# Layer 0's output products moved into layer 1, and the gates spread by sixteen transfers to every sixteenth partition

## The chip, the cores and the metric

The kernel runs on one core of one Trainium2 chip. The metric is the time of one execution on the device, in microseconds (us). Of three runs of the kernel before the median is 1395.56 us (1394.31 to 1398.51). The profile is of a further execution, which took 1393.95 us.

Names of engines: PE is TensorE (PEld its weight loads), DVE is VectorE, ACT is ScalarE, POOL is GpSimd. SP is SyncE, which issues nearly all of this kernel's transfers (SPq marks the issuing instructions).

## What is computed

A network of four layers on x of 8 batches of 512 tokens of 128 channels, in fp32. Each layer adds an attention-like block and a feed-forward block to x, each after a layer norm. The change touches the feed-forward block of layer 0, a mixture of experts for each head of each token:

```python
def _L0_ffn_ref(x, Wm, bm, expert_emb, W1, b1, W2, b2, Wo, bo):
    H, E, K = (8, 16, 2)                      # heads, experts, experts kept
    h = x @ Wm + bm
    t = h.reshape(bs * L_ * H, HD)            # HD = 16 channels a head
    w = softmax(t @ expert_emb)
    topw, topi = top_k(w, K)
    hmid = gelu(einsum('td,edi->tei', t, W1) + b1)
    eo = einsum('tei,eio->teo', hmid, W2) + b2
    comb = (take(eo, topi) * topw).sum(axis=1)
    return comb.reshape(bs, L_, d) @ Wo + bo

x = x + _L0_ffn_ref(_layernorm(x), ...)
```

The kernel computes all 16 experts for every token and multiplies each with a gate, the softmax weight where the expert is among the best two and zero elsewhere. Layer 1 is linear attention with a gated feed-forward and a few chosen tokens, layers 2 and 3 follow; the change does not touch what they compute.

## The kernel before

The residual lies in SBUF as x0 to x7, one tile for each batch. The program is written out by hand in order (`tc.manual_schedule`): what the code issues first on an engine runs first there, and an instruction that waits holds up everything behind it on its engine. SP is such a queue too. Each transfer that SP issues also waits until the transfer eight before it on SP has landed, so at most eight are under way.

**Phase A** (to about 100 us) is layer 0's attention and the preparation of its experts: two software pipelines over the eight batches (`run`, L498 to L535), each a list of stages with a lag. `scale(b, own)` (L343) applies a layer norm to the four 128-token tiles of a batch, `own` of them on ACT and the rest on POOL; the second list calls it with all four on ACT (L520). `logits` and `exponentials` (L440) write the exponentials of the softmax into the accumulator `acc` of the batch, which is free at that time.

**Gates.** `choice(b)` (L442 to L481) makes the gates of a batch on DVE in 13 steps, transposes them and writes them to DRAM as `gates[b]`, 128 rows (8 heads by 16 experts) of 512 tokens, in four transfers of 64 KB (L477). `spread(b, k)` (L543 to L554) reads the gates of experts 4k to 4k+3 back into a tile `gs` of 128 partitions by 4 experts by 512 tokens. In SBUF the partitions are 8 heads of 16 channels, so each head's 8 KB (4 experts by 512 tokens) goes to 16 neighbouring partitions. That is one transfer for each head: eight transfers of 16 partitions by 8 KB, 128 KB each. The first spread of all, (0, 0), is cut in two by experts and has sixteen transfers of 64 KB. The tile has three buffers. There are 32 spreads of 1 MB, four for each batch; `fetch` (L666) issues the next one when its batch's gates are written and the buffer three back has been used.

**Units.** The 128 pairs (batch, expert) are units. `first_half` (L556) makes four matmuls `ps<-h,w` and the Gelu on ACT (L569 of 512 columns, L570 of 1536). `second_half` (L573), issued two units later, makes four matmuls `ps<-hm,w`, then DVE `pr = (ps + b2) * gs` (L582), then POOL `acc += pr` (L588; expert 0 writes `acc` directly). Of the last unit of all, `pr` is kept instead of added. Between units `side` (L650) puts one piece of other work: a step of the next batch's `choice`, or of the index places and first norms of layer 1.

**Finish.** `finish(b)` (L590) multiplies a batch's `acc` with `wo` (four matmuls `ps<-blob_f,acc` at L250, in `by_token`) and adds the product to x on DVE (L274, `add_to_residual`). In the loop over units it stands in the unit of expert 4 of the next batch, between that unit's first half and the second half of the one two before, and takes its PSUM bank from one of the two three-bank tiles (`threes`) that the first halves use in turn. The last one, `finish(7)`, stands behind the loop and has eight matmuls, since it adds the kept `pr` as a second term.

**Layer 1** follows at once: a pipeline over i = 0 to 7 of the stages at L1217 to L1238, each with a lag, so that batch i + lag is worked on. `stats` has lag 2, `scale` lag 1, `project_q` and `project_kv` lag 0. A tile `nought` of zeros (L1253) is written to two DRAM buffers at the layer's start (L1256, L1261). Layers 2 and 3 come after it.

Of the kernel before, what the change touches and what calls it, by code (L numbers as in the profile page):

```python
# [25 lines left out]
P = 128  # L26
D = 128
# [137 lines left out]
def body(ctx, tc, dram, spans, x_in, ib, it, ic, ei, out):  # L165
# [111 lines left out]
        return t[:, j * P : (j + 1) * P]  # L277


    def layer0():  # L280


# [5 lines left out]
        with ExitStack() as st:  # L288
# [4 lines left out]
            emb = once.tile([P, 8, 16], F32, tag="emb", name="emb")  # L293
            emb_f = emb.rearrange("p h e -> p (h e)")
            h = once.tile([P, NB, TB], F32, tag="h", name="h")
            acc = once.tile([P, NB, TB], F32, tag="acc", name="acc")
            depth = once.tile([P, NB, TB], F32, tag="depth", name="depth")
            gates = [tc.dram_tile([P, TB], F32, name=f"gates{b}") for b in range(NB)]
            G = J * 8
# [40 lines left out]
            def stats(b):  # L340
                l0[b]["by"] = stats_of(x[b], J)

            def scale(b, own=3):  # L343
                l0[b]["xn"] = xn = norm.tile([P, J, D], F32, tag="xn", name="xn")
                nb, rs = l0[b]["by"]
                scaled(xn, x[b], (nb, rs), own)
                for j in range(own, J):
                    r1, n1 = rs[:, j : j + 1], nb[:, j : j + 1]
                    nc.gpsimd.tensor_scalar(xn[:, j, :], x[b][:, j, :], r1, n1, ALU.mult, ALU.add)

            def biased(b, bias):
                nc.gpsimd.tensor_tensor(
# [84 lines left out]
                nc.vector.tensor_tensor(by_expert(depth, b), pl3, over(mx), ALU.subtract)  # L437

            def exponentials(b):
                nc.scalar.activation(acc[:, b, :], depth[:, b, :], AF.Exp)  # L440

            def choice(b):  # L442


                d, ex = by_expert(depth, b), by_expert(acc, b)
                place, top, sm = small("place"), small("top"), small("sm")
                eq, one, left = big("eq"), big("one"), big("left")
                nc.vector.scalar_tensor_tensor(eq, d, 0.0, rank, ALU.is_equal, ALU.mult)
                yield "V"
                nc.vector.tensor_reduce(place, eq, AX.X, ALU.max)  # L450
                yield "V"
                nc.vector.tensor_tensor(one, eq, over(place), ALU.is_equal)
                yield "V"
                nc.vector.scalar_tensor_tensor(left, one, -1e30, d, ALU.mult, ALU.add)
                yield "V"
                nc.vector.tensor_reduce(top, left, AX.X, ALU.max)
                yield "V"
                nc.vector.tensor_tensor(eq, left, over(top), ALU.is_equal)
                nc.gpsimd.tensor_tensor(eq, eq, rank, ALU.mult)
                yield "V"  # L460
                nc.vector.tensor_reduce(sm, ex, AX.X, ALU.add)
                nc.vector.reciprocal(sm, sm)
                nc.gpsimd.tensor_tensor(ex, ex, over(sm), ALU.mult)
                yield "V"
                nc.vector.tensor_reduce(place, eq, AX.X, ALU.max)
                yield "V"
                nc.vector.tensor_tensor(one, eq, over(place), ALU.is_equal)
                yield "V"
                nc.vector.scalar_tensor_tensor(left, one, -1e30, left, ALU.mult, ALU.add)
                yield "V"  # L470
                nc.vector.scalar_tensor_tensor(left, left, -1e29, ex, ALU.is_le, ALU.mult)
                yield "V"
                g = big("turned").rearrange("p g e -> p (g e)")
                nc.vector.transpose(g, left.rearrange("p g e -> p (g e)"))
                to = gates[b].rearrange("(c r) (j a s) -> a r j c s", c=4, j=J, a=4)
                for a in range(4):
                    nc.sync.dma_start(  # L477
                        to[a], g[32 * a : 32 * (a + 1), :].rearrange("r (j c s) -> r j c s", j=J, c=4)
                    )
                written.add(b)  # L480
                yield "V"  # L481
# [7 lines left out]
            with (  # L489
                tc.tile_pool(name="a0h", bufs=1) as hp,  # L490
                tc.tile_pool(name="a0", bufs=2) as ap,
                psum({"one": 8}),
                tc.manual_schedule(),
            ):
                hs = [hp.tile([P, NB, TB], F32, tag=f"h{k}", name=f"h{k}") for k in range(3)]
                bst = [hp.tile([P, NB, 6], F32, tag=f"bst{k}", name=f"bst{k}") for k in range(3)]

                def run(stages, iterations):  # L498
                    for i in iterations:
                        for f, lag in stages:  # L500
                            if 0 <= i + lag < NB:
                                f(i + lag)

                run(
                    (
                        (scale, 2),
                        (stats, 3),
                        (turned, 1),
                        (project, 0),
                        (lambda b: biased(b, "bp"), -2),  # L510
                    ),
                    range(-3, NB + 2),
                )
                keep_clock(22)
                sc, bi = batch_norm()
                expand()
                run(
                    (
                        (turned, -2),
                        (lambda b: scale(b, J), -1),  # L520
                        (turn_v, 3),
                        (logits, -3),
                        (attended, 0),
                        (stats, 0),
                        (spikes, 4),
                        (gram, 2),
                        (gram_out, 1),
                        (hidden, -2),
                        (exponentials, -3),
                        (lambda b: chosen(3), -4),  # L530
                        (lambda b: biased(b, "bo"), -1),
                        (lambda b: keep_clock(6), -3 - NB // 2),
                    ),
                    range(-4, NB + 3),
                )  # L535
                chosen(20)
# [6 lines left out]
            def spread(b, k):  # L543

                gs = wp.tile([P, 4, TB], F32, tag="gs", name="gs", bufs=3)
                src = gates[b].rearrange("(h k e) t -> k h e t", h=8, k=4)[k]
                n = 2 if (b, k) == (0, 0) else 4
                for e in range(0, 4, n):
                    for hd in range(8):
                        nc.sync.dma_start(  # L550
                            gs[16 * hd : 16 * (hd + 1), e : e + n, :],
                            src[hd, e : e + n, :].unsqueeze(0).to_broadcast([16, n, TB]),
                        )
                return gs  # L554

            def first_half(b, e):  # L556
# [16 lines left out]
            def second_half(b, e, hm, gs):  # L573
                po = bank()
                for i in range(4):
# [2 lines left out]
                        w2[:, e, :, :].rearrange("p a o -> p (a o)"),  # L578
                        hm[:, i, :],
                    )  # L580
                pr = acc[:, b, :] if e == 0 else wp.tile([P, TB], F32, tag="pr", name="pr")
                nc.vector.scalar_tensor_tensor(  # L582
                    pr, po, f0["b2"][:, e : e + 1], gs, ALU.add, ALU.mult
                )
                if (b, e) == (NB - 1, 15):
                    l0[b]["last"] = pr
                elif e > 0:
                    nc.gpsimd.tensor_tensor(acc[:, b, :], acc[:, b, :], pr, ALU.add)  # L588

            def finish(b):  # L590
                terms = [(lambda j: acc[:, b, j * P : (j + 1) * P], f0["wo"])]
                if "last" in l0[b]:
                    terms.append((lambda j: cols(l0[b]["last"], j), f0["wo"]))
                add_to_residual(b, by_token(terms, None))

            def places():

# [45 lines left out]
            with tc.manual_schedule():  # L643
# [36 lines left out]
                def second(n):  # L680

                    if n >= 2:
                        b, e = units[n - 2]
                        second_half(b, e, hms.pop(n - 2), gs[(n - 2) // 4][:, e % 4, :])
                        fetch(n - 1)
                    for _ in range(1 if n > 1 else 5):
                        side("V", n)

                for n in range(len(units) + 2):
                    first(n)  # L690
                    if n >= len(units):

                        banks["own"] = threes[0][:, 1 + n - len(units), :]
                        second(n)
                        banks.pop("own")
                        continue

                    banks["own"] = threes[(n + 1) % 2][:, 0, :]
                    b, e = units[min(n, len(units) - 1)]
                    if e == 4 and b > 0:  # L700
                        finish(b - 1)
                    else:
                        side("P", n)
                    banks.pop("own")
                    second(n)
                finish(NB - 1)
                n = 1000
                while kinds.get(1) != "end":
                    side("V", n)
# [121 lines left out]
    def layer1():  # L831
# [9 lines left out]
        with tc.tile_pool(name="l1", bufs=2) as wp, tc.tile_pool(name="l1c", bufs=1) as once:  # L841
# [372 lines left out]
            def chosen_put():  # L1214
# [11 lines left out]
                (f_scale, -3),  # L1226
                (q_map, 0),
                (project_kv, 0),
                (z_turn, -7),
                (output, -2),  # L1230
                (k_map, 0),
# [7 lines left out]
            with tc.manual_schedule():  # L1239
# [10 lines left out]
                for k, name in enumerate(("eb1", "eb2")):  # L1250
                    lo, hi = spans["rows"][name]
                    nc.sync.dma_start(ebs[:, k, :], dram["rows"][:, lo:hi].partition_broadcast(P))
                nought = once.tile([P, J, D], F32, tag="nought", name="nought")  # L1253
                nc.gpsimd.memset(nought, 0.0)
                for b in range(1, NB):
                    nc.sync.dma_start(  # L1256
# [1421 lines left out]
```

## Time and profile before

| what | us |
|---|---|
| median of three runs | 1395.56 |
| the profiled execution | 1393.95 |
| its span in the trace | 1392.2 |
| first transfer of spread (0, 0) is issued | 97.8 |
| last transfer of the last spread is issued | 364.9 |
| last gating on DVE (L582) starts | 383.76 |
| first matmul of layer 1 | 386.24 |
| one iteration of layer 1 | 7.49 |

The span is what the trace covers. All times inside the kernel are counted from its start. A line of a group gives the code line, engine, operation and tiles (output, then inputs), the count, and behind it the busy time, the mean of one in ns, and the idle time of the engine just before with what ended it. In a view by stretches each engine has its busy time in the stretch; behind them stand the granted PE clock, the mean busy share of the 16 DMA engines and the GB/s that they moved. The granted clock of PE is full over the whole span (0.998 on average).

The unit stage lies between about 102 and 386 us. One unit takes 2.07 us there, and a batch of 16 takes 34.06 us (the first) to 34.9 us, with one unit of 3.49 us in each, the one that holds a `finish`.

### The profile page before, as it was taken

The page shows a single profiled execution, that of the slowest core. Times are in us where ns is not written, and L with a number is a line of the kernel's source. Part 1 is how long each engine was busy: PE and PEld are TensorE (multiplying, and loading weights), DVE is VectorE, ACT ScalarE, POOL GpSimd, SP SyncE. Part 2 cuts the span into 40 slices and gives each one's busy share as a digit, 9 for nine tenths or more (in the row PEclk, how much of TensorE's full clock was granted, in tenths as well). Part 3 has the DMA queues.
Part 4 walks back from the last instruction along what each step waited for, and adds up shares of the span by engine and source line. Part 5 has one row for each costly group of instructions (what it writes and reads, how often), then busy time and mean ns, then how long its engine had stood idle before and what let it go on. Part 6 is the DMA issues. An engine that isn't in the chain of part 4 may idle for free.

```text
span 1392.2 us, 33106 instructions
## 1 busy us (share of the span) xinstructions
PE 1327.5 (95%) x12935; PEld 706.1 (51%) x12935; DVE 1014.3 (73%) x2148; ACT 1014.6 (73%) x2060; POOL 642.4 (46%) x748
## 2 busy tenths in 40 slices
PE   7889999999989999999999999999999999999997
PEld 3762222222267655547447545555555545555576
DVE  6785556666467778863783778888788797887876
ACT  7869999999978656665684686787767867667632
POOL 6645666666632533330472353353443634424432
PEclk9999999999999999999999999999999999999999
DMA  5019999999681010031211101101011010010000
GB/s 180 1 27 139 141 126 127 132 127 133 85 272 32 28 40 24 16 108 33 60 31 38 45 2 22 30 2 33 20 22 24 9 33 20 19 27 9 2 8 16
DMA packets 100713, 78.14 MB, mean 56 GB/s; under 512 B 52717, under 2 KB 93581, under 8 KB 96206
## 3 DMA queue, kind: packets, MB, share of 16 engines
q1 hardware_dynamic: 98828, 72.10, 28.3%
q0 software_dynamic: 1152, 2.36, 0.6%
q8 instruction: 102, 1.67, 0.6%
q10 hardware_dynamic: 578, 1.57, 0.3%
q14 instruction: 53, 0.43, 0.1%
HBM read 59.03 MB, written 16.97 MB: 55 GB/s over the span
## 4 chain that ended last, share of the span: by engine, by line
PE 52%; ACT 22%; DVE 19%; issue 3%; POOL 2%; DMA 1%; SPq 1%; DVEq 0%; ACTq 0%; POOLq 0%
PE ps L250 41%; PE ps L1556 8%; ACT hm L570 6%; ACT ex L1635 5%; DVE nm L1629 5%; ACT hm L569 3%; ACT prod L2023 2%; PE ps L2206 1%; DVE fa L1395 1%; DVE acc L2009 1%; DVE s L732 1%; ACT h L389 1%; DVE fa L1379 1%; DVE fsc L1374 1%; ACT q L1517 1%
## 5 line engine op out<-in xcount | busy, mean ns | idle before, releaser
L1635 ACT ACTIVATE ex<-ps,nm 128x512 f32<-128x512 f32 x512 | 345.2, 687 | 172.6 <-DVE nm L1629 170.2
L1629 DVE TENSOR_REDUCE nm<-ps 128x2 f32<-128x1024 f32 x256 | 301.1, 1211 | 41.9 <-PE ps L250 41.5
L250 PE MATMUL ps<-q,k 64*64 64x512 f32 (+1 forms) x2240 | 258.3, 565 | 7.4 <-ACT ex L1635 5.4
L250 PE MATMUL ps<-ex,vs 128*64 128x512 f32 x1024 | 233.9, 599 | 1.1 <-DVE sm L1649 1.1
L1650 POOL TENSOR_TENSOR vs<-v,sm 128x256 f32<-128x256 f32 x128 | 78.6, 614 | 296.6 <-DVE sm L1649 269.6
L588 POOL TENSOR_TENSOR acc<-acc,pr 128x512 f32<-128x512 f32 x119 | 165.6, 1391 | 93.8 <-DVE pr L582 85.8
L1556 PE MATMUL ps<-xt,blob_a 64*64 64x512 f32 x912 | 207.8, 589 | 0.5 <-SPq L1523 0.5
L570 ACT ACTIVATE hm<-ps,blob_f 128x1536 f32<-128x1536 f32 x128 | 196.2, 1533 | 0.0
L582 DVE SCALAR_TENSOR_TENSOR pr<-ps,blob_f,gs 128x512 f32<-128x512 f32 x120 | 90.1, 750 | 93.7 <-PE ps L250 72.1
L250 PEld LDWEIGHTS ps<-q,k 64*64 64x64 f32 x2240 | 74.6, 132 | 150.5 <-ACT ex L1635 77.6
L250 PE MATMUL ps<-h,w 32*128 32x512 f32 x1024 | 148.3, 643 | 1.1 <-ACT hm L569 0.6
L250 PEld LDWEIGHTS ps<-ex,vs 128*64 128x64 f32 x1024 | 68.1, 137 | 152.9 <-issue 126.7
L250 PE MATMUL ps<-hm,w 128*32 128x512 f32 x1024 | 136.9, 607 | 2.3 <-DVE pr L582 2.2
L2024 POOL TENSOR_TENSOR acs<-acs,prod 128x512 f32<-128x512 f32 x96 | 124.0, 1292 | 23.9 <-ACT prod L2023 19.4
L1556 PE MATMUL ps<-blob_a,ct 64*64 64x128 f32 x1824 | 118.6, 269 | 0.0
L1556 PE MATMUL ps<-blob_a,xt 64*64 64x128 f32 x1824 | 118.6, 269 | 0.0
L1556 PEld LDWEIGHTS ps<-blob_a,ct 64*64 64x64 f32 x1824 | 106.3, 133 | 0.0
L1635 ACT ACTIVATION_READ_ACCUMULATOR ex<-ps,nm 128x1 f32 x512 | 104.9, 205 | 0.0
L1556 PEld LDWEIGHTS ps<-blob_a,xt 64*64 64x64 f32 x1824 | 103.0, 133 | 0.0
L569 ACT ACTIVATE hm<-ps,blob_f 128x512 f32<-128x512 f32 x128 | 88.0, 687 | 13.3 <-PE ps L250 13.2
L250 PEld LDWEIGHTS ps<-h,w 32*128 32x128 f32 x1024 | 41.0, 184 | 109.1 <-ACT hm L569 100.5
L1556 PEld LDWEIGHTS ps<-xt,blob_a 64*64 64x64 f32 x912 | 61.7, 133 | 32.2 <-issue 28.7
(373 smaller groups left out, 2204.5 us busy)
## 6 DMA issues: line engine op xcount, KB each, us to landing
gs<-gates SPq DMA_DIRECT2D x248, 128.0 KB, 7.4
ht<-turned_h SPq DMA_DIRECT2D x20, 180.0 KB, 3.0
turned_h<-hb SPq DMA_DIRECT2D x40, 88.0 KB, 2.3
blob_f<-in_f SPq DMA_DIRECT2D x1, 2560.0 KB, 9.0
blob_a<-in_a SPq DMA_DIRECT2D x1, 2056.0 KB, 13.5
x<-in_x SPq DMA_DIRECT2D x8, 256.0 KB, 5.8
gates<-turned SPq DMA_DIRECT2D x32, 64.0 KB, 4.7
slots_in<-nought SPq DMA_DIRECT2D x8, 256.0 KB, 4.8
```

Source lines behind the costliest of these rows:

```text
L250: nc.tensor.matmul(out_, lhs, rhs, start=start, stop=stop)
L389: nc.scalar.activation(hk, hk, AF.Sigmoid, bias=bi[:, k : k + 1], scale=sc[:, k : k + 1])
L569: nc.scalar.activation(hm[:, 0, :], p1, AF.Gelu, bias=bias)
L570: nc.scalar.activation(hm[:, 1:, :], p3, AF.Gelu, bias=bias)
L582: nc.vector.scalar_tensor_tensor(pr, po, f0["b2"][:, e : e + 1], gs, ALU.add, ALU.mult)
L588: nc.gpsimd.tensor_tensor(acc[:, b, :], acc[:, b, :], pr, ALU.add)
L1556: ins = nc.tensor.matmul(*args, **kw).ins
L1629: nc.vector.tensor_reduce(nm, ps, AX.X, ALU.max, negate=True)
L1635: nc.scalar.activation(ex[kt][:, i, :], ps[:, i, :], AF.Exp, bias=nm[:, i : i + 1], accum_out=sm[:, kt, i : i + 1],)
L1650: nc.gpsimd.tensor_tensor(vs[:, tiles, :, :], vs_[n][:, tiles, :].rearrange("p j (i n) -> p j i n", i=2), sm[:, tiles, :].unsqueeze(3).to_ ...
L2023: nc.scalar.activation(p, src, AF.Copy, scale=w)
L2024: nc.gpsimd.tensor_tensor(t["acs"], t["acs"], p, ALU.add)
```

## The change

It has five parts, all in one diff.

1. `acc` is no longer one tile of layer 0. Batches 0 to 2 have tiles of their own there; batches 3 to 7 share `last_acc` in a pool that lives through layer 1. `finish` is defined outside layer 0. The kept `pr` of the last unit is gone: POOL adds it to `acc` as for any unit, and every `finish` has four matmuls.
2. In the unit loop only `finish(0)` and `finish(1)` remain. `finish(2)` stands behind the second half of unit 126, in the drain of the loop. `finish(3)` to `finish(7)` are a stage of layer 1 with lag 3, behind `project_kv`.
3. A spread, other than (0, 0), is sixteen transfers in place of eight. Transfer r takes the same 64 KB of all eight heads, and puts head j's 8 KB on partition r + 16 j: eight partitions of 8 KB, 64 KB. SP's issues of gates rise from 264 to 512 (16 and 496).
4. `scale` in phase A's second list puts three of the four tiles on ACT and the fourth on POOL, as the first list does.
5. In the first two units four and two pieces of `side` work run in place of five and five. `nought` takes its buffer from a tile of another name.

```diff
+    acc = []
+    last_acc = first.tile([P, NB - 3, TB], F32, tag="acc", name="acc")
+
+    def finish(b):
+        wo = f0["wo"]
+        add_to_residual(b, by_token([(lambda j: cols(acc[b], j), wo)], None))
+
     def layer0():
...
-            acc = once.tile([P, NB, TB], F32, tag="acc", name="acc")
+            acc.extend(once.tile([P, TB], F32, tag=f"acc{b}", name="acc") for b in range(3))
+            acc.extend(last_acc[:, b, :] for b in range(NB - 3))
...
-                        (lambda b: scale(b, J), -1),
+                        (scale, -1),
...
                 src = gates[b].rearrange("(h k e) t -> k h e t", h=8, k=4)[k]
-                n = 2 if (b, k) == (0, 0) else 4
-                for e in range(0, 4, n):
-                    for hd in range(8):
-                        nc.sync.dma_start(
-                            gs[16 * hd : 16 * (hd + 1), e : e + n, :],
-                            src[hd, e : e + n, :].unsqueeze(0).to_broadcast([16, n, TB]),
-                        )
+                if (b, k) == (0, 0):
+                    for e in (slice(0, 2), slice(2, 4)):
+                        for hd in range(8):
+                            nc.sync.dma_start(
+                                gs[16 * hd : 16 * (hd + 1), e, :],
+                                src[hd, e, :].unsqueeze(0).to_broadcast([16, 2, TB]),
+                            )
+                else:
+                    for r in range(16):
+                        nc.sync.dma_start(gs[r::16, :, :], src)
...
-                if (b, e) == (NB - 1, 15):
-                    l0[b]["last"] = pr
-                elif e > 0:
-                    nc.gpsimd.tensor_tensor(acc[:, b, :], acc[:, b, :], pr, ALU.add)
+                if e > 0:
+                    nc.gpsimd.tensor_tensor(acc[b], acc[b], pr, ALU.add)
...
-                    for _ in range(1 if n > 1 else 5):
+                    for _ in range((4, 2)[n] if n < 2 else 1):
                         side("V", n)
...
                     if n >= len(units):
-                        banks["own"] = threes[0][:, 1 + n - len(units), :]
+                        if n > len(units):
+                            banks["own"] = bank("first")
                         second(n)
+                        if n == len(units):
+                            banks["own"] = threes[0][:, 0, :]
+                            finish(2)
                         banks.pop("own")
                         continue
...
-                    if e == 4 and b > 0:
+                    if e == 4 and 0 < b < 3:
                         finish(b - 1)
...
-                finish(NB - 1)
...
                 (project_kv, 0),
+                (lambda b: b > 2 and finish(b), 3),
                 (z_turn, -7),
...
-                nought = once.tile([P, J, D], F32, tag="nought", name="nought")
+                nought = wp.tile([P, J, D], F32, tag="zo", name="nought")
```

More of the change, by code (lines that the diff above doesn't have):

```diff
@@ L341, in stats, with scale @@
                 l0[b]["by"] = stats_of(x[b], J)
-            def scale(b, own=3):
+            def scale(b):
                 l0[b]["xn"] = xn = norm.tile([P, J, D], F32, tag="xn", name="xn")
                 nb, rs = l0[b]["by"]
[L346 to L349, printed above, removed]
+                scaled(xn, x[b], (nb, rs), 3)
+                r1, n1 = rs[:, 3:4], nb[:, 3:4]
+                nc.gpsimd.tensor_scalar(xn[:, 3, :], x[b][:, 3, :], r1, n1, ALU.mult, ALU.add)
             def biased(b, bias):
@@ L439, in exponentials @@
             def exponentials(b):
-                nc.scalar.activation(acc[:, b, :], depth[:, b, :], AF.Exp)
+                nc.scalar.activation(acc[b], depth[:, b, :], AF.Exp)
             def choice(b):
-                d, ex = by_expert(depth, b), by_expert(acc, b)
+                d = by_expert(depth, b)
+                ex = acc[b].rearrange("p (g e) -> p g e", e=16)
                 place, top, sm = small("place"), small("top"), small("sm")
@@ L580, in second_half @@
                     )
-                pr = acc[:, b, :] if e == 0 else wp.tile([P, TB], F32, tag="pr", name="pr")
+                pr = acc[b] if e == 0 else wp.tile([P, TB], F32, tag="pr", name="pr")
                 nc.vector.scalar_tensor_tensor(
@@ L584, in second_half @@
                 )
-                if (b, e) == (NB - 1, 15):
-                    l0[b]["last"] = pr
-                elif e > 0:
-                    nc.gpsimd.tensor_tensor(acc[:, b, :], acc[:, b, :], pr, ALU.add)
[L590 to L594, printed above, removed]
+                if e > 0:
+                    nc.gpsimd.tensor_tensor(acc[b], acc[b], pr, ALU.add)
             def places():
```

## The prediction

> **What bounds the kernel now.** I read the groups and the chain first, then the stretches of the unit stage, then the waits of SP. The change lies in the unit stage (102 to 386 us) and its neighbours.
>
> ```profile
> PE 52%; ACT 22%; DVE 19%; issue 3%; POOL 2%; DMA 1%; SPq 1%; DVEq 0%; ACTq 0%; POOLq 0%
> ...
> L570 ACT ACTIVATE hm<-ps,blob_f 128x1536 f32<-128x1536 f32 x128 | 196.2, 1533 | 0.0
> L582 DVE SCALAR_TENSOR_TENSOR pr<-ps,blob_f,gs 128x512 f32<-128x512 f32 x120 | 90.1, 750 | 93.7 <-PE ps L250 72.1
> ```
>
> DMA is 1% of the chain, ACT sits before L570 for nothing, and DVE before L582 waits mostly for PE: transfers are hidden. A unit lasts 2.07 us, about what L570's 1.53 us and L569's 0.69 us take on ACT less their overlap. How well hidden, the stretches tell (the columns are PE, PEld, DVE, ACT, POOL, granted clock, DMA share, GB/s):
>
> ```profile
> 13.00:14.00 1.00, 1.00 (x3) 0.48 (x2) 0.00 (x0) 1.00 (x3) 0.92 (x1) 1.00 1.04 439
> 15.00:16.00 1.00, 1.00 (x3) 0.33 (x2) 0.33 (x1) 0.57 (x1) 0.00 (x0) 1.00 1.04 440
> 200.00:240.00 40.00, 39.69 (x312) 9.82 (x312) 27.79 (x54) 38.35 (x37) 27.33 (x21) 1.00 0.98 130
> 280.00:320.00 40.00, 39.45 (x308) 9.71 (x304) 28.02 (x55) 38.34 (x37) 27.69 (x22) 1.00 0.99 129
> ```
>
> PE, ACT and the DMA engines are all full in the unit stage. But the 16 engines move 130 GB/s there, while the loads over 128 partitions at the start get 440. So the engines are busy because each packet is slow: at 440/16 = 27.5 GB/s an engine moves 8 KB in 0.30 us, at 130/16 = 8.1 GB/s in 1.0 us, 3.4 times as long. The early loads contain one that every partition reads from the same row (blob_bc), so it isn't the repeated reading; what differs is that each transfer goes to 16 neighbouring partitions. Now SP's waits (total us, times, longest):
>
> ```profile
> SPq L550 <- DMA gs<-gates: 84.8, 129, 1.8
> ...
> SPq L550 <- DMA gates<-turned: 20.5, 18, 3.1
> SPq L550 <- DVE pr L582: 16.2, 13, 2.2
> ```
>
> SP mostly waits for older spread transfers, little for a free buffer. A spread is 1 MB and takes 8 x 1.0 = 8 us against 8.28 us of four units, and at each of 7 batch boundaries it pauses 20.5/7 = 2.9 us for the gates to land in DRAM. So per batch the transfers need 4 x 8 + 3 = 35 us, just the batch period (34.06 to 34.9). The DMA stands level with PE and ACT: there is no slack to spend.
>
> **Part by part.**
>
> *Finishes out of the loop.* In the timeline at 215.8 us the unit that holds a finish starts its L569 at 215.82, the next L569 comes at 219.30: 3.48 us against 2.07, a bubble of 1.41.
>
> ```profile
> 216.01 1.13 PE L250 MATMUL ps<-blob_f,acc 128*128 128x128 f32 x8 [0.29 <-ACT hm L570]
> ...
> 217.25 0.69 DVE L274 TENSOR_TENSOR x<-x,ps 128x512 f32<-128x512 f32 x1 [1.18 <-PE ps L250]
> 218.07 0.31 PEld L250 LDWEIGHTS ps<-h,w 32*128 32x128 f32 x8 [0.84 <-DVE x L274]
> ...
> 219.30 0.69 ACT L569 ACTIVATE hm<-ps,blob_f 128x512 f32<-128x512 f32 x1 [1.37 <-PE ps L250]
> ```
>
> The next first half waits for L274 to free the borrowed bank, behind it ACT. Five of seven such bubbles go: 5 x 1.42 = -7.1 us, if nothing else is late. What is late next is the transfers.
>
> *The tail.* finish(7), eight matmuls with a 0.72 us wait on POOL, held PE from 383.6 to 386.2. It leaves, finish(2) fills part of the drain: -2.7 us (0 if layer 1's start must wait for x2 anyway).
>
> *In layer 1.* Each of five finishes is four matmuls of 0.275 us with hidden loads, about 1 us of PE, and an L274 of 0.69 us on DVE. An iteration lasts 7.49 us with PE 9.56, ACT 9.87 and DVE 8.76 us busy in 10 (420 to 430 us). PE's 4% gaps cover little. I take 0.8 each, +4 us (0 if the gaps hold it, 5.5 if L274 in front of layer 1's DVE work delays it too). New wait: L274 waits for PE, and stats and feature maps queue behind it on DVE.
>
> *Phase A.* Eight tiles of 0.48 us move from ACT to POOL (0.45 each). In 60 to 75 us ACT is busy 14.4 of 15 us, POOL 11.2. -1 us (-2.5, all on the path for half, to +1, if the turn waits for POOL). The other moves (zero tile, four and two side steps) are hidden by PE and ACT being full: 0 (within 1 us either way).
>
> *The spread*, which decides. 496 transfers of 64 KB, eight packets of 8 KB, replace 248 of 128 KB. Three prices are needed.
>
> Engines: a transfer's rows are dealt out one to an engine. In the queue rows,
>
> ```profile
> q10 hardware_dynamic: 578, 1.57, 0.3%
> ```
>
> 578 is four blobs of 128 rows and one of a single row (513), and 65 completions, 4 x 16 + 1: the one-row transfer used one engine. So I take eight engines for eight rows, and as all transfers start from the first, the same eight.
>
> Issue: SP's eight back-to-back issues at 163.40 take 3.56 us, 0.45 each; with sixteen, 7.3 us a spread, under 8.28. It fits, barely.
>
> Time of a transfer: at the lone pace of a packet 0.30 us, so SP's 0.46 is the low end; the high end is today's packet, 1.0 us, if a packet to its partition is slow by itself. Between: today 16 engines write to 16 neighbours and each is slowed 3.1 to 3.4 times, as if about four shared one way in. If strided partitions share as neighbours do, eight engines are slowed half as much. In proportion that is 1.0/2 = 0.50; in whole sharers it is two, 2 x 0.30 = 0.60. Today's successive transfers go to different heads and can overlap, which may be why 3.4 and not 4 is seen; new successive ones go next door to each other. So I take 0.60, nearest to half of today's row, on its slow side; 0.52 to 0.65 for this case.
>
> [...]
>
> **Sum.** A spread then takes 16 x 0.60 = 9.6 us, a batch 4 x 9.6 + 3.5 (today's 2.9 pause and 0.6 to fill up) = 41.9 against 33.1 of compute: the stage is bound by DMA. Transfers after (0, 0) flow from about 107.6 (97.8 and sixteen issues and landing). 107.6 + 31 x 9.6 + 7 x 3.5 + 2 (landing) = 432. The last spread is gated by four units, the first of which now starts when its data is there; drain 3.5: layer 1 starts at 435.5 in place of 386.24, +49. The bubbles and the tail are inside this, hidden by the transfers. With +4 and -1 it is +52: 1393.95 + 52 = 1446. The profiled run lies 1.6 under the median of the runs, so I say 1447. With 0.52, -40; with 0.65, +25: 1407 to 1472.
>
> **Rivals.**
> 1. *Strided partitions don't share, and the transfers stay hidden* (not slower). For: half as many engines are at work at once, and 440 GB/s is reached over all partitions. Against: no row shows strided targets. The same sum gives no change at 0.495 us a transfer, so it decides there. At SP's 0.46, with 5.7 us of SP per boundary (issue of gates, landing, refill): 106.4 + 496 x 0.463 + 7 x 5.7 + 2.3 = 378.3, layer 1 at 381.8, -4.4 + 4 - 1: about 1393. If SP issues a little faster, compute binds: -7.1 - 2.7 + 4 - 1 = -6.8: 1387. Chance 0.21 (0.12 faster, 0.09 the same).
> 2. *The total stays at 128 to 130 GB/s*, 0.51 us a transfer: 107.6 + 253 + 24.5 + 2 + 3.5 = 390.6, +4.4 + 4 - 1 = +7: 1402. For: the transfer total is what today's rows measure. Chance 0.16.
> 3. *A packet keeps its 1.0 us, on half the engines*: 15 us a spread at 0.94, +220: about 1614. For: the change would have cut the engines at work to half. Against: 3.4 times the lone packet needs sharers. Chance 0.08.
>
> **The numbers.** The forecast has 0.55; faster and same come from rival 1, all else is slower. About 0.3% is what measurement can tell from no change. Chances: faster 0.12, same 0.09, slower 0.79. The range takes in rivals 1 and 2 and the forecast's own range, and leaves rival 3 out: 1387 to 1472.
>
> **What would show it.** Right: in the unit stage the DMA share falls to about one half at 100 to 115 GB/s, batch periods near 42 us, DVE L582 waiting for DMA gs (now 4.5 us in all) by tens of us, gaps before ACT L569 in most units, layer 1's first matmul near 435. Wrong: a DMA share near 1 (16 engines for eight rows), GB/s at 130 or above, SP waiting for DVE pr (a free buffer) rather than for its own transfers, and periods of 33 us. The finish part by itself is right if the units of 3.48 us are gone from all but two batches and layer 1's iterations grow by 0.8 us; phase A, if the first unit starts about 1 us earlier.

## The result, and the profile after

The changed kernel takes 1456.21 us (median of five runs, 1452.7 to 1458.29), the kernel before 1396.26 us (five runs): a ratio of 1.0428, 95% interval 1.041 to 1.0446. The forecast was 1447 us. The profiled execution took 1452.7 us, with a span of 1450.9 us.

Where the time went, from the starts of the same instructions in both traces (us; the last column is the fastest version, told of below):

| stretch | before | after | a_r8 |
|---|---|---|---|
| start to first L427 `h<-ps` (L434 after) | 62.2 | 61.1 | 61.0 |
| to the first Gelu | 40.9 | 40.5 | 40.5 |
| first to last short Gelu: the units | 276.6 | 335.0 | 266.6 |
| last short Gelu to layer 1's first matmul | 6.5 | 5.8 | 5.3 |
| layer 1, first `xt,blob_l` to last `blob_l,zt` | 112.7 | 116.6 | 120.3 |
| the rest, layers 2 and 3 | 893.3 | 892.0 | 892.5 |

All of the loss is in the units. (a_r8's layer 1 has 3 us more than the 117.1 of a_r4, the same code there; its profile shows a granted clock of 0.66 in one 10 us stretch. The stretch ahead of the first L427 differs by up to 1.9 us between profiles of kernels with the same code there, so it says nothing.)

First the stretches of the unit stage in the changed kernel, with the columns of before (PE, PEld, DVE, ACT, POOL, granted clock, DMA share, GB/s):

```profile
200.00:240.00 40.00, 33.30 (x252) 7.61 (x248) 19.70 (x32) 31.91 (x31) 21.98 (x16) 0.95 0.38 105
240.00:280.00 40.00, 33.53 (x252) 7.18 (x248) 18.88 (x32) 33.22 (x32) 23.61 (x17) 0.93 0.37 105
280.00:320.00 40.00, 35.20 (x256) 7.72 (x256) 21.36 (x41) 33.31 (x32) 23.63 (x17) 0.95 0.38 106
```

PE and ACT, full before, are idle for about a sixth of the time. The GB/s fell from 130 to 105. The DMA share is 0.38, three quarters of the 0.50 that eight of 16 engines make up: the engines are not full. (Between 200 and 320 us never more than eight packets of 8 KB overlap in its trace; before, 16 to 18 do for 89 of the 120 us. The granted PE clock is 0.93 to 0.95 in these stretches, 1.00 before.) Now SP's waits in the stage (100 to 440 us), its issues of gates (before, then after), and a piece of its timeline:

```profile
SPq L564 <- DMA gates<-turned: 10.6, 17, 0.9
SPq L201 <- ACT hm L581: 2.9, 1, 2.9
SPq L564 <- DVE pr L593: 2.3, 6, 0.6
```

```profile
L550 SPq DMA_DIRECT2D gs<-gates x264: 302/328/2118, 97.8 to 364.9; - x132
L564 SPq DMA_DIRECT2D gs<-gates x496: 542/543/1436, 105.2 to 433.0; - x166
```

```profile
177.63 2.65 SPq L485 DMA_DIRECT2D gates<-turned  x4
181.92 38.46 SPq L564 DMA_DIRECT2D gs<-gates  x64
220.47 2.65 SPq L485 DMA_DIRECT2D gates<-turned  x4
```

The wait of SP for its own older transfers, 84.8 us before, is gone. SP doesn't wait for anything much: it issues. (The numbers behind the count are the shortest, median and longest issue in ns.) One issue has a median of 0.543 us where it was 0.328, and 64 in a row take 38.46 us, 0.60 each. A batch is 38.46 + 2.65 for the gates' own writes + 1.64 until they have landed = 42.8 us, and batch periods are 39.6 to 43.6. So what ends last in the changed kernel is SP's issuing, and the unit's gating waits for it. DVE's waits for gates, two lines of before (102 to 386 us) and three of after (102 to 440 us), then the groups of the page, the first line of before and the others of after:

```profile
DVE pr L582 <- DMA gs<-gates: 3.7, 3, 1.3
DVE acc L582 <- DMA gs<-gates: 0.8, 3, 0.3
...
DVE acc L593 <- DMA gs<-gates: 43.8, 8, 6.5
DVE pr L593 <- DMA gates<-turned: 11.4, 6, 2.7
DVE pr L593 <- DMA gs<-gates: 10.4, 8, 2.8
```

```profile
L569 ACT ACTIVATE hm<-ps,blob_f 128x512 f32<-128x512 f32 x128 | 88.0, 687 | 13.3 <-PE ps L250 13.2
...
L581 ACT ACTIVATE hm<-ps,blob_f 128x1536 f32<-128x1536 f32 x128 | 196.3, 1533 | 0.0
...
L593 DVE SCALAR_TENSOR_TENSOR pr<-ps,blob_f,gs 128x512 f32<-128x512 f32 x120 | 90.0, 750 | 120.5 <-PE ps L250 89.7
...
L580 ACT ACTIVATE hm<-ps,blob_f 128x512 f32<-128x512 f32 x128 | 88.0, 687 | 71.2 <-PE ps L250 71.1
```

The first unit of each batch (`acc`, expert 0) bears most of it, 43.8 us in 8 waits. The idle time before the short Gelu (L569, now L580) rose from 13.3 to 71.2 us, 57.9 of the 58.4 us that the units lost. The page's chain doesn't reach the units: it breaks off where layer 1 ends (at 559 us). That of b_strided below, which has the same spread, does.

### The profile page after: what moved, and what is told of

Read it like the earlier page. It is cut to its first block, busy times and chain, and to the rows that moved or that the text cites. A ratio compares the mean times of both kernels' runs of the same rounds, so it can differ in the third digit from the quotient of the medians.

```text
span 1450.9 us, 33333 instructions
## 1 busy us (share of the span) xinstructions
PE 1342.2 (93%) x12927; PEld 707.3 (49%) x12927; DVE 1012.9 (70%) x2148; ACT 1012.9 (70%) x2052; POOL 648.4 (45%) x757
## 4 chain that ended last, share of the span: by engine, by line
PE 34%; DVE 15%; ACT 9%; issue 2%; POOL 1%; DMA 0%; SPq 0%; DVEq 0%; ACTq 0%; POOLq 0%
PE ps L250 24%; PE ps L1562 7%; ACT ex L1641 5%; DVE nm L1635 5%; ACT prod L2029 2%; DVE acc L2015 1%; PE ps L2212 1%; DVE fa L1401 1%; DVE fa L1385 1%; DVE fsc L1380 1%; ACT q L1523 1%; DVE k L1524 1%; DVE fa L1402 1%; ACT xn L1460 1%; DVE fm L1400 1%
## 5 line engine op out<-in xcount | busy, mean ns | idle before, releaser
L250 PE MATMUL ps<-hm,w 128*32 128x512 f32 x1024 | 146.2, 645 | 51.4 <-DVE acc L593 37.7
L250 PE MATMUL ps<-h,w 32*128 32x512 f32 x1024 | 154.9, 670 | 1.1 <-ACT hm L580 0.6
L580 ACT ACTIVATE hm<-ps,blob_f 128x512 f32<-128x512 f32 x128 | 88.0, 687 | 71.2 <-PE ps L250 71.1
L250 PEld LDWEIGHTS ps<-hm,w 128*32 128x32 f32 x1024 | 20.7, 111 | 152.1 <-DVE pr L593 90.8
```

Source lines behind the costliest of these rows:

```text
L250: nc.tensor.matmul(out_, lhs, rhs, start=start, stop=stop)
L580: nc.scalar.activation(hm[:, 0, :], p1, AF.Gelu, bias=bias)
```

## The experiments

The theory after the result: the stage is bound by the transfers of gates, and it is SP's issuing of strided transfers (0.60 us) that paces them. The rival is the prediction's own reason: strided partitions share a way in, and a transfer takes 0.60 us by itself. Both give the same time. A third question is whether the moved finishes gave anything.

**Which part costs the time.** Two kernels exchange the spread alone.

b_strided is the kernel before with

```diff
-                n = 2 if (b, k) == (0, 0) else 4
-                for e in range(0, 4, n):
-                    for hd in range(8):
-                        nc.sync.dma_start(gs[16 * hd : 16 * (hd + 1), e : e + n, :], ...)
+                    for r in range(16):        # (0, 0) as before
+                        nc.sync.dma_start(gs[r::16, :, :], src)
```

> The kernel before with the new spread alone. If the spread is the whole loss, the time is about that of the changed kernel, 1450 to 1460 us: layer 1 starts near 442 us, with the seven bubbles hidden behind the transfers. If the moved finishes carry part of the loss, it is 10 us or more below 1450.

Measured: 1455.35 us (four runs; before 1396.41 beside it), ratio 1.042 (1.0402 to 1.0437). The spread alone is the whole loss. SP has 8% of this kernel's chain, 1% in that of before. Between 140 and 300 us the chain runs in each batch along SP's issues of the first spread, through their landing, to the gating of expert 0, and for the rest of the batch mostly along PE. One such place:

```profile
181.02 0.60 SPq L556
...
189.75 0.54 SPq L556
...
190.33 2.62 DMA gs<-gates
...
193.07 0.76 DVE acc L585
```

a_neigh is the changed kernel with

```diff
-                    for r in range(16):
-                        nc.sync.dma_start(gs[r::16, :, :], src)
+                    for hd in range(8):
+                        nc.sync.dma_start(gs[16 * hd : 16 * (hd + 1), :, :],
+                                          src[hd, :, :].unsqueeze(0).to_broadcast([16, 4, TB]))
```

> The changed kernel with the spread of before: eight transfers of 128 KB to 16 neighbouring partitions. All other parts of the change stay. If transfers were level with compute before (8 us a spread, 35 us a batch with the pause for the gates), the five bubbles of 1.42 us are not gained: batch periods stay at 34.5 to 35 us, and the time is 1392 to 1397 us (phase A -1.5, tail -2.7, layer 1 +3.9). If the bubbles were on the path by themselves, periods of batches without a finish fall to about 33.1 us and the time is 1385 to 1389 us.

Measured: 1399.43 us (seven runs), ratio 1.002 (1.0006 to 1.0034): no gain from the moved finishes. Batch periods are 34.5 to 36.9 us. SP's waits (100 to 390 us), then the longest of DVE's for gates (102 to 390 us):

```profile
SPq L564 <- DMA gs<-gates: 107.1, 155, 1.8
SPq L564 <- DMA gates<-turned: 25.0, 17, 3.8
...
DVE acc L596 <- DMA gs<-gates: 13.0, 6, 3.1
```

The bubbles are gone and the transfers take their place: SP's wait for its own older transfers grew from 84.8 to 107.1 us, and DVE's for gates in all from 4.5 to 16.8 us. The time is 2 us over what was expected at most; layers 2 and 3, which nothing here touches, took 2 us more in this profile than in that of before.

**What an issue costs.** Four kernels hold one thing and change another. a_half carries half the bytes, and the gates of two experts serve for all four:

```diff
-                        nc.sync.dma_start(gs[r::16, :, :], src)
+                        nc.sync.dma_start(gs[r::16, 0:2, :], src[:, 0:2, :])
...
-                        second_half(b, e, hms.pop(n - 2), gs[(n - 2) // 4][:, e % 4, :])
+                        second_half(b, e, hms.pop(n - 2), gs[(n - 2) // 4][:, e % 4 if n < 6 else e % 2, :])
```

> The changed kernel, but each strided transfer carries half the bytes: 8 partitions of 4 KB, gates of experts 4k and 4k+1 alone, which are used for 4k+2 and 4k+3 too (so the gates of half the experts are other ones). The count and form of the issues stay. Theory issue (SP needs 0.60 us for each strided issue, and that paces): 1450 to 1458 us, nothing gained. Theory data (the prediction's: two packets share a way in, 0.60 us for 64 KB): the transfers halve to 0.30 us and hide: 1385 to 1397 us.

Measured: 1464.35 us (two runs), ratio 1.0486 (1.0463 to 1.0509). Half the bytes gain nothing: as the issue theory has it. (It is 8 us longer than the changed kernel; the units have 4.6 us of that, layers 2 and 3 some 3, and why is not settled.) SP's issues have the same median, at 54 to 56 GB/s:

```profile
L564 SPq DMA_DIRECT2D gs<-gates x496: 542/543/1435, 107.0 to 439.9; - x166
```

a_neigh16 holds the count, sixteen, and takes the form of before:

```diff
-                    for r in range(16):
-                        nc.sync.dma_start(gs[r::16, :, :], src)
+                    for e in (0, 2):
+                        for hd in range(8):
+                            nc.sync.dma_start(gs[16 * hd : 16 * (hd + 1), e : e + 2, :],
+                                src[hd, e : e + 2, :].unsqueeze(0).to_broadcast([16, 2, TB]))
```

> The changed kernel with sixteen transfers of 64 KB a spread, as many as in the change, but each to 16 neighbouring partitions (two experts of one head, 16 rows of 4 KB). If it is the form (strided target and source) that makes an issue cost 0.60 us: issue 0.45 us, 7.2 us a spread, about the time of a_neigh, 1392 to 1400 us. If it is the count alone (any issue at this rate costs 0.58 us or more): 1450 us or more.

Measured: 1404.37 us (three runs), ratio 1.0052 (1.0031 to 1.0073), 4 us over the most that was expected and 5 over a_neigh. The issue has a median of 418 ns. Sixteen issues a spread alone lose little; it is their form.

a_src1 and a_dst8 tell source from target.

```diff
-                        nc.sync.dma_start(gs[r::16, :, :], src)
+                        # a_src1
+                        nc.sync.dma_start(gs[r::16, :, :],
+                                          src[r // 2, :, :].unsqueeze(0).to_broadcast([8, 4, TB]))
+                        # a_dst8
+                        nc.sync.dma_start(gs[8 * r : 8 * (r + 1), :, :], src)
```

> The changed kernel, with sixteen transfers to every sixteenth partition as in the change, but each reads the 8 KB of one head alone for all eight partitions (so the gates on seven of eight heads are another head's). The target stays strided, the source is one row. If the strided source makes the issue dear: SP's issue falls from 0.54 to 0.30 to 0.42 us, and the stage with it: 1390 to 1405 us, as a_neigh16; if the strided target makes it dear: 0.54 us, 1450 to 1460 us. And if SP issues faster, theory data is tried at its own place: two packets sharing would hold 0.60 us a transfer, SP would wait for its own older transfers, and the time would stay near 1450 us.

> The mirror: sixteen transfers, each reads the eight rows of 8 KB as in the change, but puts them on eight neighbouring partitions (so most partitions get another head's gates). Source strided, target not. If the source makes the issue dear: 0.54 us, 1450 to 1460 us. If the target does: 0.30 to 0.42 us, and then 1390 to 1405 us unless the neighbours' sharing holds the transfers (about half of today's 1.0 us for half the bytes, 8 us a spread).

Measured: a_src1 1454.24 us, a_dst8 1495.85 us (two runs each). Their issues, a_src1 first, then a_dst8:

```profile
L564 SPq DMA_DIRECT2D gs<-gates x496: 542/543/1563, 105.6 to 434.2; - x166
```

```profile
L564 SPq DMA_DIRECT2D gs<-gates x496: 262/263/1263, 106.0 to 475.8; - x166
```

Of these sixteen transfers of 64 KB, the target makes the issue dear: strided, 0.543 us even with a one-row source; eight neighbours, 0.263 us even with a strided source. My time for a_dst8 with a cheap issue (1390 to 1405, unless sharing holds it) missed, and it is the condition that came true:

```profile
SPq L564 <- DMA gs<-gates: 162.1, 349, 1.1
```

SP waits for its own older transfers, the DMA share is 0.50 to 0.53 throughout, and the stage moves 93 GB/s (110 to 480 us; its stretches of 40 us between 72 and 116). So to eight neighbouring partitions fewer bytes went in a second than to eight partitions 16 apart, which got 105 to 109 GB/s with the engines as full (a_pair between 200 and 360 us, below).

**What the transfer costs.** a_src1 left the data theory untried, since its issue stayed dear. a_pair tries it: the same partitions, half as many issues, each with twice the bytes.

```diff
-                gs = wp.tile([P, 4, TB], F32, tag="gs", name="gs", bufs=3)
...
+                pair[0] = wp.tile([P, 8, TB], F32, tag="gs", name="gs", bufs=2)   # even k
...
+                both = gates[b].rearrange("(h k e) t -> k h e t", h=8, k=2)[k // 2]
-                        nc.sync.dma_start(gs[r::16, :, :], src)
+                        nc.sync.dma_start(pair[0][r::16, :, :], both)
```

> The changed kernel with half as many strided transfers, each twice as large: a tile of gates holds eight experts (two buffers), and a spread of eight experts is sixteen transfers to every sixteenth partition of 8 partitions by 16 KB, 128 KB. The pattern on the partitions is that of the change, bytes are the same, issues are halved. If only the issue paces the changed kernel: 9.6 us of SP for eight units of 16.5 us, hidden, 1387 to 1395 us. If strided partitions also share, at the prediction's 0.60 us for 64 KB (1.20 here): 19.2 us for eight units and 42 us a batch with the pause, 1440 to 1450 us; at 0.55 us, two lone packets' 0.30 less what overlaps, 17.6 us and some 38 us a batch, 1412 to 1425 us.

Measured: 1458.65 us (two runs), ratio 1.0441 (1.0411 to 1.0472). So halving the issues gains nothing either. (It is 9 us over what was expected of shared transfers: the first batch took 53.6 us, counted between the gatings of expert 0, the others 39.3 to 42.9, near the 42 foretold.) Its stretches, then SP's waits (100 to 440 us):

```profile
200.00:240.00 40.00, 36.33 (x264) 9.54 (x264) 20.71 (x33) 30.43 (x30) 22.21 (x16) 0.88 0.49 109
240.00:280.00 40.00, 36.28 (x264) 7.91 (x256) 19.75 (x32) 33.52 (x33) 23.97 (x18) 0.91 0.49 109
```

```profile
SPq L575 <- DMA gs<-gates: 78.9, 131, 1.2
SPq L575 <- DMA gates<-turned: 27.4, 17, 4.9
```

Now SP waits for its own transfers (78.9 us), the DMA share is 0.49, eight of 16 engines full, and 109 GB/s over eight engines is 13.6 each, half of the lone 27.5. A packet of 16 KB has a median of 1.20 us in the trace between 200 and 320 us, twice the 0.60 us that its bytes take at the lone pace, and the fastest of them in the stage took 0.608: it isn't the longer row that is slow, it is as if two shared a way in. The tile has two buffers of eight experts in place of three of four, and SP waits 10.9 us for a free one; but with the engines full from 200 to 360 us, other buffers would not have moved more. So a 64 KB transfer of the change needs 0.60 us of eight full engines and 0.60 us of SP: two limits at one place, and taking away either leaves the other. In the changed kernel itself SP is the one that is met: its 8 KB packets have a median of 0.43 us between 200 and 320 us, more than the lone 0.30 and less than the 0.60 that full engines would give (half of a_pair's 1.20).

**Taking away both.** a_r8 has eight transfers a spread; each reads all eight heads and writes each head to two partitions, every eighth partition in all. a_r4, a_r2 and a_one go on to four, two and one.

```diff
-                    for r in range(16):
-                        nc.sync.dma_start(gs[r::16, :, :], src)
+                    rows = src.rearrange("h e t -> h (e t)")
+                    for r in range(8):                     # a_r4: 4, a_r2: 2, a_one: 1
+                        to = gs[r::8, :, :].rearrange("p e t -> p (e t)")
+                        nc.sync.dma_start(to, rows.unsqueeze(1).to_broadcast([8, 2, 4 * TB]))
```

> The changed kernel with eight strided transfers a spread in place of sixteen: transfer r reads the same 64 KB of all heads and puts each head's 8 KB on two partitions (every eighth partition, 16 partitions, 128 KB). Theory issue: eight issues of 0.60 us are 4.8 us a spread, well under 8.28 us, and unless the transfers themselves are slow the stage is bound by compute: batch periods of 33.1 us, 1385 to 1392 us. Theory data (strided partitions share as neighbours do, about 1 us for 128 KB on eight engines or more): 9 to 10 us a spread, 1440 us or more.

> The same with four transfers of 256 KB a spread, to every fourth partition (32 partitions). Theory issue: 2.4 us of SP a spread, 1385 to 1392 us; if an issue costs by its rows (32 in place of 8), about 2.4 us each, 9.6 us a spread, near 1450 us.

> The same with two transfers of 512 KB a spread, to every second partition. Theory issue: 1385 to 1392 us; cost by rows: near 1450 us. If eight engines with four or more rows each are the limit (8 rows x 0.30 us at best, 4.8 us a spread), it is still hidden; a landing only at the end of a whole half spread might be late for the first unit after the gates, up to 2 us a batch.

> The same with one transfer of 1 MB a spread to all 128 partitions. Theory issue: SP nearly idle, 1385 to 1392 us; cost by rows: near 1450 us. At eight engines' lone pace the spread takes 16 x 0.30 = 4.8 us; at 130 GB/s 8 us, then 1393 to 1400.

Measured, beside 1395.83 us of before:

| kernel | us (runs) | ratio, 95% | SP per issue, ns | mean 8 KB packet, us |
|---|---|---|---|---|
| a_r8 | 1388.11 (5) | 0.9949, 0.9931 to 0.9967 | 575 | 0.37 |
| a_r4 | 1388.93 (3) | 0.9953, 0.9933 to 0.9972 | 575 | 0.38 |
| a_r2 | 1389.42 (8) | 0.9952, 0.9937 to 0.9966 | 577 | 0.43 |
| a_one | 1401.18 (8) | 1.003, 1.0002 to 1.0057 | 608 | 0.52 |

(The packets are those between 200 and 320 us; before has 0.96 there, the changed kernel 0.43.) a_r8 beats both kernels, the one before by 0.5%. Its stretches and issues:

```profile
200.00:240.00 40.00, 40.00 (x316) 9.23 (x312) 24.15 (x39) 40.00 (x40) 28.84 (x21) 1.00 0.43 141
240.00:280.00 40.00, 40.00 (x316) 9.06 (x312) 27.27 (x51) 40.00 (x39) 28.96 (x23) 1.00 0.42 134
```

```profile
L566 SPq DMA_DIRECT2D gs<-gates x248: 574/575/1272, 105.3 to 352.6; - x124
```

ACT and PE are busy for 40.00 of 40 us, and batches without a finish take 33.05 to 33.3 us: bound by compute. An issue costs 0.575 to 0.577 us for 16, 32 or 64 partitions, hardly more than the 0.543 for eight, so "cost by rows" falls. Most of a_r8's packets have the lone time (median 0.309 us): these strided targets hardly share. a_one lies 1 us over the last branch of its expectation (1393 to 1400, at 8 us a spread): eight engines (the DMA share is 0.48 to 0.50) at 0.52 us a packet need 16 x 0.52 = 8.3 us for a spread, level with compute once more, and the runs spread from 1391 to 1408 us. Why packets grow slower from eight transfers to one (0.37 to 0.52 us) isn't settled.

**What the finishes are worth.** b_r8 is the kernel before with a_r8's spread.

> The kernel before with the spread of a_r8 alone (eight strided transfers of 128 KB); finishes, the layer norm's tiles and the rest as before. With transfers off the path the seven bubbles still cost 1.42 us each: batch periods of 33.07 + 1.42 = 34.5 us, and against a_r8 +7.1 (five bubbles) +1.2 (drain) +0.5 (phase A) -2.6 to -3.9 (layer 1): 1393 to 1395 us, 0.1 to 0.2% under before. If the lighter transfers alone were the gain of a_r8, it is 1387 to 1390 us.

Measured: 1396.28 us (eleven runs), ratio 1.0007 (0.9996 to 1.0018): nothing gained, 1 to 3 us above what was worked out. With a_neigh it makes a table of two by two (us; the kernels with moved finishes hold the other parts of the change too, of which phase A's is worth 0.5 us):

| | spread of before | spread of a_r8 |
|---|---|---|
| finishes in the loop | 1396.3 | 1396.3 (b_r8) |
| finishes moved | 1399.4 (a_neigh) | 1388.1 (a_r8) |

b_r8's profile shows the bubble alone, with DMA out of the way (share 0.39 to 0.42):

```profile
216.60 0.69 DVE L274 TENSOR_TENSOR x<-x,ps 128x512 f32<-128x512 f32 x1 [1.18 <-PE ps L250]
217.41 0.31 PEld L250 LDWEIGHTS ps<-h,w 32*128 32x128 f32 x8 [0.84 <-DVE x L274]
218.65 0.69 ACT L574 ACTIVATE hm<-ps,blob_f 128x512 f32<-128x512 f32 x1 [1.37 <-PE ps L250]
```

The kernel before was bound twice, by the bubbles and by the transfers, and each hid behind the other. Moving the finishes pays only with transfers that are light, and light transfers pay only with the finishes moved.

## Why the prediction was right, point by point

- *The stage becomes bound by the transfers of gates, periods near 42 us, PE and ACT idle.* Right in the periods (39.6 to 43.6 us) and the 105 GB/s. But "bound by DMA" isn't what the trace shows: the share is 0.38, foretold about one half, and SP doesn't wait for its own transfers, it issues them.
- *0.60 us a transfer, two sharers.* Right in size where the engines are full, as a_pair shows (1.20 us for a packet of 16 KB, twice the lone 0.60). In the changed kernel it is not the step that ends last: the packets took 0.43 us.
- *"Issue: SP's eight back-to-back issues at 163.40 take 3.56 us, 0.45 each; with sixteen, 7.3 us a spread, under 8.28. It fits, barely."* This step failed. An issue with a strided target costs 0.543 us and 0.60 in a row, 9.6 us a spread; the row that I took had another form. Had the data been fast, the kernel would still have lost, as a_half did. The forecast came out right with one of its two limits unseen, because both are 0.60: that is luck.
- *Rival 1, strided partitions don't share.* It fails for every sixteenth partition (a_pair, 1.20 us a packet) and holds nearly for every eighth (a_r8's packets have a median of 0.309 us): a_r8's 1388.1 is the 1387 that the rival gave for a stage bound by compute.
- *Bubbles: 5 x 1.42 us if nothing else is late.* Right: the gain is hidden in the change and in a_neigh; with a_r8 the units take 266.6 us against 276.2 in b_r8, 9.7 less, the five bubbles' 7.1 and 2.6 more that no run takes apart.
- *Layer 1: +4 us.* Measured +3.9 (112.7 to 116.6), but only 2.6 of it up to the start of the eighth iteration, behind the last finish: four of the five iterations with a finish take 8.1 us and the second 7.5, as one without. So a finish costs about 0.5 us, not 0.8, and that the sum fits is luck; where the other 1.3 us come from is open. The first finish and the fourth in the timeline after:

```profile
445.03 1.05 PE L250 MATMUL ps<-blob_f,acc 128*128 128x128 f32 x8
...
446.73 0.68 DVE L274 TENSOR_TENSOR x<-x,ps 128x512 f32<-128x512 f32 x1
...
469.76 0.69 DVE L274 TENSOR_TENSOR x<-x,ps 128x512 f32<-128x512 f32 x1 [0.42 <-PE ps L250]
```

  At the first, nothing stands still (no idle time is marked); before the L274 of the other four DVE waits 0.42 us for PE, the new wait that was foretold.
- *Phase A: -1 us.* Measured -0.46, from the first L427 to the first Gelu (40.9 to 40.5, in all kernels with the edit).
- *Layer 1 starts at 435.5.* It started at 442.3. The last issue began at 433.0, so its data came some 3 us later than the 432 of the sum, and the drain was mis-sized: the first of the last four gatings starts at 436.1 and layer 1 at 442.3, 6.2 us for what I took as 3.5. Of the tail's -2.7 us, from the last short Gelu to layer 1, 0.7 came (6.5 to 5.8), and 1.2 in a_r8. The last four gatings start at 436.1, 438.5, 440.5 and 442.6, a unit's time apart; the drain does not close up.

## What to carry to other kernels

Where a queue both issues transfers and has to keep pace, take the cost of an issue from a row of the very form that is added, and count issues as a resource beside bytes. When a change moves work off one limit, look whether another stands level with it: here neither half of the remedy gained anything alone, and a test that takes away one cause and sees no gain has not cleared that cause. And when a transfer's pattern is changed, the number of rows in one transfer and which partitions they hit are two dials: eight transfers to every eighth partition kept issues and sharing low at once (a_r8: 8 x 0.575 = 4.6 us of issues a spread, packets of 0.37 us).

## What was not expected of the hardware

- An issue on SP cost by the form of its target: 0.26 us (a_dst8) to 0.33 us (before) for eight or 16 neighbouring partitions with 8 KB rows, 0.54 to 0.58 us for strided ones, whatever the bytes (4 to 16 KB a row: a_half, the change, a_pair) and nearly whatever the rows (8 to 64: the change, a_r8, a_r4, a_r2). a_one's target is not strided and cost 0.61 us, with a source that repeats each of eight rows 16 times, so a stride is not the only thing that makes it dear.
- With eight engines full, transfers of eight rows to eight neighbouring partitions moved 93 GB/s over the stage (a_dst8, its stretches between 72 and 116) and to every sixteenth partition 105 to 109 (a_pair, in rows of 16 KB). To every eighth it was 131 to 141 with the engines not full, where the compute set the pace (a_r8).
